# Attention and FP4 FFN kernel: the FFN input of two tiles is quantized as one, block-transposed on VectorE and moved by transfers

## The chip, the core and the metric

The kernel runs on one core of one Trainium2 chip, as one launch. The metric is the device time of that launch in microseconds (us). Three runs before the change took 3573.21, 3571.87 and 3572.76 us; the median is 3572.76 us.

## What is computed

The reference is one transformer block on 8 sequences of 1024 rows and 512 columns, in float32. A layer norm, causal attention in a latent form (16 heads of 32 columns, 16 further columns that are rotated by position) and a residual sum come first. Then come a second layer norm and a gated FFN of 1408 hidden columns, of which every input and every weight is rounded to a 4-bit grid with one scale for each 16 consecutive columns:

```
def fp4_quant_dequant(x):
    xb = x.reshape(shape[:-1] + (shape[-1] // BLOCK, BLOCK))     # BLOCK = 16
    scale = jnp.max(jnp.abs(xb), axis=-1, keepdims=True) / 6.0
    scale = jnp.maximum(scale, jnp.float32(1e-12))
    idx = jnp.searchsorted(_MID, jnp.abs(xb / scale))
    q = _GRID[idx] * jnp.sign(xb / scale) * scale
...
gate = fp4_linear(x, w_gate)
y = fp4_linear(x, w_up)
h = jax.nn.silu(gate) * y
return fp4_linear(h, w_down)
...
x = x + attention(layernorm(x))
x = x + ffn(layernorm(x))
```

## The kernel before

**Two streams of work.** Attention runs in 16 units of 512 rows (two per sequence, four tiles of 128 rows each). An even unit has three score steps per group of four heads, an odd unit seven, and there are four groups. `score_step` (L577) lays the matmuls of one step, ScalarE's exponentials (L618), the clamp of the first half on VectorE (L633) and of the second on GpSimd (L636), and for steps on the diagonal the causal mask on GpSimd (L640). The sums over steps are made on VectorE (L662). At the end of a unit `out_proj` (L779) multiplies by w_o, which `fetch_wo` (L775) loads anew each time into a buffer that score steps use too, adds x and writes the tile to a buffer in DRAM (`mid`).

The FFN runs in 32 pairs of two tiles. Of pair m: `fetch` (L813) loads y, one tile at a time, from `mid`; `begin` (L817) takes the norm's statistics; `scaled` (L822) norms a tile on ScalarE and queues its quantization; `turned` (L828) turns a tile with four matmuls against an identity matrix (L835) and ScalarE copies the result into two yT tiles (L840). Then six `gate` and six `up` pieces (L861, L881) run over the hidden columns, 256 at a time and 128 in the last, with yT as the moving operand (L853); `down` (L901) multiplies the quantized h by w_down and `finish` (L923) adds the residual and stores.

**Quantization.** `quantize` (L201) takes parts of up to 512 columns: a block maximum (L214), six small operations on the scales (L230 to L235), and per part six passes (L254, L262, L265, L268 twice, L250). With `turned` set, as for h, whose blocks of 16 lie along the partitions, it also transposes blocks of 32 x 32 on VectorE before and after (L224).

**Attention's own input** already goes another way in most units: `settle` (L390) transposes 32 x 32 blocks of xp on VectorE (L393) and 16 transfers of 32 partitions move the blocks to their places in xnT (L398). The planner counts 13 us for them.

**Order.** TensorE, VectorE and ScalarE run in the order in which the source lays instructions (`manual_schedule`, L78); GpSimd and SP, which issues nearly all transfers, are ordered by the framework's scheduler. The class `Clock` keeps the author's estimates of each engine's time. `slack` (L132) queues VectorE's quantization steps, `fill` puts them where the planner expects VectorE to be idle, and `need` (L102) forces the steps of one key out.

`ffn_pieces` (L930) is a list of pieces, each with a cost. A unit takes pieces up to a budget and spreads them between its score steps; units 13 and 14 have 22 us taken off their budget:

```
budget = within * (13, 5)[u % 2 == 0] / left
if u in (n_units - 3, n_units - 2):
    budget -= 22.0
```

What is left goes to unit 15. Pair 30 and pair 31 need unit 15's output, so they, and most of pair 29, run after all attention; that stretch is called the tail here. yT and h tiles share a ring of nine buffers, and y tiles have two.

Of the kernel before, what the change touches and what calls it, by code (L numbers as in the profile page):

```python
# [18 lines left out]
P = 128  # L19
# [23 lines left out]
def tile_mla_then_fp4_ffn(  # L43
# [31 lines left out]


    ET = mybir.EngineType
    ctx.enter_context(tc.manual_schedule(engines={ET.PE, ET.DVE, ET.Activation}))  # L78

    class Clock:  # L80

# [92 lines left out]
    xls.update({t: load_x(0, t, p2, "y") for t in range(2, NT)})  # L174
    by_chunk = lambda w: w.rearrange("(c p) n -> p c n", p=P)
    by_head = lambda w: w.rearrange("p (h n) -> p h n", n=64)
    of_four = lambda w: w.unsqueeze(0).to_broadcast([4, *w.shape])
# [20 lines left out]
        on_act(0.56, lambda: nc.scalar.copy(dst, pt[:, 0:n, :]))  # L198


    def quantize(parts, key, turned=False, ready=0.0):  # L201

        ends, at = [], 0
        for part in parts:
# [30 lines left out]
            nc.vector.reciprocal(rs, sc)  # L235

        for k, part in enumerate(parts):
            if turned:
                turn_blocks(part)
            slack(0.06 + 0.0012 * part.shape[1], lambda k=k: amax(k), key, ready=ready)  # L240
        slack(1.1 + 0.008 * nb, scales, key)
        for part, end in zip(parts, ends):
            step, bl = part.shape[1], slice(*end)
            nbl = step // BLK
            part3 = part.rearrange("p (b k) -> p b k", k=BLK)

            def times(which, part3=part3, bl=bl, nbl=nbl):
                by = got[which][:, bl].unsqueeze(2).to_broadcast([P, nbl, BLK])
                if which == "sc":
                    nc.vector.tensor_tensor(part3, part3, by, ALU.mult)  # L250
                else:


                    nc.vector.scalar_tensor_tensor(  # L254
                        part3, part3, BELOW_ONE, by, ALU.mult, ALU.mult
                    )

            def steps(part=part, step=step):  # L260
# [12 lines left out]
            slack(pass_cost, lambda f=to_grid: f(ALU.add), key)  # L273
            slack(pass_cost, lambda f=to_grid: f(ALU.subtract), key)
            slack(pass_cost, lambda f=times: f("sc"), key)
            if turned:
                turn_blocks(part)


# [297 lines left out]
    def score_step(u, hq, j, qc, qr, acc, aT):  # L577
# [46 lines left out]
        while silus:  # L624
            silus.popleft()()

        for k, (half, ready) in enumerate(zip(halves, done)):
            part = pT[:, half, :cols]
            if k == 0:
                on_dve(  # L630
                    0.1 + 0.00062 * wide,
                    ready,
                    lambda: nc.vector.tensor_scalar(part, part, E_HI, E_LO, ALU.min, ALU.max),  # L633
                )
            else:
                nc.gpsimd.tensor_scalar(part, part, E_HI, E_LO, ALU.min, ALU.max)  # L636
            if masked:

                diag = pT[:, half, : len(segs) * P].rearrange("p h (n k) -> p h n k", k=P)
                nc.gpsimd.affine_select(  # L640
                    out=diag,
                    in_=diag,
                    pattern=[[0, 2], [0, len(segs)], [1, P]],
                    compare_op=ALU.is_ge,
                    fill=0.0,
                    base=0,
                    channel_multiplier=-1,
                )
        ready = clk.act + 0.4 + 0.0009 * wide + (0.7 if masked else 0.0)


# [158 lines left out]
    NS = (NFC + 1) // 2  # L810
    ys, yTs, hs, ends = {}, {}, {}, {}

    def fetch(n):  # L813
        ys[n] = p2.tile([P, D], F32, tag="y", name=f"y_{n}")
        nc.sync.dma_start(out=ys[n], in_=mids[tiles[n]])

    def begin(*ns):  # L817
        for n in ns:
            stats, ends[n, "y"] = normed(ys[n], ("y", n))
            slack(0.9, stats, ("ny", n), True, clk.pe + 2.0)  # L820

    def scaled(n):  # L822
        clk.need(("ny", n), pe=False)
        clk.act = max(clk.act, clk.done["ny", n] + 2.5)
        on_act(0.65, ends.pop((n, "y")))
        quantize([ys[n]], ("y", n), ready=clk.act)

    def turned(n):  # L828
        m, t = divmod(n, 2)
        clk.need(("y", n))  # L830
        if t == 0:
            yTs[m] = [ring.tile([P, 2, 256], F32, tag="h", name="yT") for _ in range(2)]
        pt = bank("pt").rearrange("p (n k) -> p n k", k=P)
        for i in range(NDC):
            nc.tensor.transpose(pt[:, i, :], ys[n][:, i * P : (i + 1) * P], ident)  # L835
            clk.pe += 0.11
        ys.pop(n)
        for i in range(2):
            to = yTs[m][i][:, :, t * P : (t + 1) * P]
            on_act(0.38, lambda: nc.scalar.copy(to, pt[:, 2 * i : 2 * i + 2, :]))  # L840

    def hidden(m, w, k):

        n = min(2, NFC - 2 * k)
        pg = bank("pg").rearrange("p (n k) -> p n k", k=256)[:, :n]
        for c in range(n):
            f0 = (2 * k + c) * P
            for i in range(NDC):
                mm(
                    pg[:, c, :],  # L850
                    lhsT=w[:, i, f0 : f0 + P],
                    rhs=yTs[m][i // 2][:, i % 2, :],
                    start=(c == 0 and i == 0),  # L853
                    stop=(c == n - 1 and i == NDC - 1),
                    skip_group_check=True,
                )
        return pg
# [1 line left out]
    flat = lambda x: x.rearrange("p n k -> p (n k)")  # L859

    def gate(m, k):  # L861
        pg = hidden(m, wg_T, k)
        if k == 0:
            hs[m] = []
        if k < NS - 1:
            h = ring.tile([P, 2, 256], F32, tag="h", name="h")
        else:
            h = p1.tile([P, 1, 256], F32, tag="h_last", name="h")
        hs[m].append(h)
        copy_out(h, pg)  # L870
        if k % 2 == 1:

            def silu(hk=hs[m][k - 1 :]):
                for h in hk:
                    on_act(0.2 + 0.0009 * h.free_size(), lambda: nc.scalar.activation(h, h, AF.Silu))
                clk.silu = clk.act
                clk.act += 2.6

            silus.append(silu)

    def up(m, k):  # L881
# [8 lines left out]
        )  # L890
        for group in ((0, 1), (2, 3), (4,), (5,)) if m == pairs - 1 else ((0, 1), (2, 3), (4, 5)):
            if k == group[-1]:
                quantize([flat(hs[m][j]) for j in group], ("h", m, k // 2), True)
        if k == NS - 1:
            yTs.pop(m)

# [33 lines left out]
    def ffn_pieces():  # L930

        last = pairs - 1
        for t in range(2):
            yield 0.0, t, lambda t=t: fetch(t)
        for t in range(2):
            yield 1.0, t, lambda t=t: begin(t)
        for t in range(2):
            yield 1.0, t, lambda t=t: scaled(t)
        for t in range(2):
            yield 0.5, t, lambda t=t: turned(t)  # L940
        cost = lambda k: 3.5 if k < NS - 1 else 1.8
        for m in range(pairs):
            n = 2 * m + 1
# [6 lines left out]
            if m > 0:  # L950
                yield 0.0, n, lambda m=m: fetch_x1(2 * m - 2)
            if m < last:
                yield 0.0, n + 2, lambda n=n: fetch(n + 1)
                yield 0.0, n + 2, lambda n=n: fetch(n + 2)
            yield from run(gate, 1)
            if m < last:
                yield 0.0, n + 2, lambda n=n: begin(n + 1, n + 2)
            yield from run(up, 0, 1)
            if m < last:
                yield 0.0, n + 2, lambda n=n: scaled(n + 1)  # L960
            if m > 0:
                yield 9.6, n, lambda m=m: down(m - 1, (0,))
                yield 9.6, n, lambda m=m: down(m - 1, (1,))
            if m < last:
                yield 0.0, n + 2, lambda n=n: scaled(n + 2)
            yield from run(gate, 2, 3)
            yield from run(up, 2, 3)
            yield from run(gate, 4, 5)
            if m < last:
# [28 lines left out]
    for u in range(n_units):  # L998
# [8 lines left out]
        if u < FIRST:  # L1007
# [4 lines left out]
            for _ in range(8 if u == FIRST - 1 else 0):  # L1012
                c, n, run = ffn.popleft()
                take.append((c, run, n))
        else:
# [103 lines left out]
```

## Time and profile before

| What | Value |
|---|---|
| median of three runs | 3572.76 us |
| the profiled execution: its own time, its span | 3574.26 us, 3572.5 us |
| mean granted TensorE clock | 0.997 |
| transfers on SP's queue (q1): packets, share of 16 engines | 187780, 13.5% |
| yT<-pt copies on ScalarE (L840), x128 | 41.4 us, 377 ns each |
| FFN gate, up and down matmuls, busy | 640.3, 639.7 and 617.9 us |
| VectorE busy from 800 to 1000 us | 91.09 and 91.82 us of each 100 |
| SP waiting for the turning matmuls (L835) before it loads y | 566.8 us, 47 times |

How to read it: the profile is one execution with every instruction timed. Busy time is the union of an engine's instructions. A line such as `L835 PE MATMUL pt<-ident,y ... x256 | 39.3, 276 | 0.1` gives the source line, engine, operation, what it writes and reads, the count, the busy us, the mean ns of one, and the idle us of the engine just before. One matmul in the program shows as two records for float32, a transpose as one. SP's busy time is not shown, since it only issues; its issues stand in the timeline.

### The profile page before, as it was taken

Reading aid. Unit: us, or ns where it says so; the run is one execution under the profiler, and the core shown is the slowest. Engines: PE = TensorE matmul, PEld = TensorE weight load, DVE = VectorE, ACT = ScalarE, POOL = GpSimd, SP = SyncE. Lnnn points to the kernel's source line nnn. Section 1 sums busy time; section 2 is a strip of 40 time slices with the busy share of each in tenths; the row PEclk is TensorE's granted clock in tenths of the full one; section 3 lists DMA queues with packets and bytes.
Section 4 is the critical chain, followed back from the end, with each engine's and each line's share of the span. In section 5 each row is a group of like instructions: output and inputs, shape, how many; then the busy total and the mean of one; then the engine's idle time right before and its main releaser. Section 6 shows DMA issues by size and latency. Waiting matters only on the chain.

```text
span 3572.5 us, 50383 instructions
## 1 busy us (share of the span) xinstructions
PE 3508.8 (98%) x19700; PEld 2016.3 (56%) x19700; DVE 2911.5 (81%) x5308; ACT 1327.7 (37%) x1850; POOL 769.6 (22%) x1086
## 2 busy tenths in 40 slices
PE   8999999999999999999999999999999999999999
PEld 4334355556655555555566555565556655555576
DVE  6778659789977889887989778898878886779987
ACT  4444443333333333333333333333343433343311
POOL 3333322112121121221221211212222122122100
PEclk9999999999999999999999999999999999999999
DMA  3212111111021101111110211011111102100100
GB/s 93 72 45 73 46 40 48 45 34 30 19 62 30 60 18 30 43 53 45 32 28 19 62 30 54 24 30 41 52 45 30 30 24 60 42 18 19 54 30 15
DMA packets 189865, 145.17 MB, mean 41 GB/s; under 512 B 126524, under 2 KB 128060, under 8 KB 189628
## 3 DMA queue, kind: packets, MB, share of 16 engines
q1 hardware_dynamic: 187780, 141.09, 13.5%
q8 instruction: 155, 2.54, 0.3%
q10 hardware_dynamic: 1848, 0.87, 0.1%
q14 instruction: 82, 0.67, 0.1%
HBM read 94.72 MB, written 33.55 MB: 36 GB/s over the span
## 4 chain that ended last, share of the span: by engine, by line
PE 70%; DVE 13%; ACT 1%; issue 1%; POOL 1%; DMA 1%; SPq 0%; ACTq 0%; DVEq 0%; POOLq 0%
PE pg L117 29%; PE pd L117 14%; PE sc_ps L117 9%; PE po L117 5%; PE num L117 5%; DVE pT L662 2%; PE pp L117 2%; DVE h L268 1%; PE den L117 1%; PE pv L117 1%; DVE h L224 1%; PE pqr L117 1%; PE pk L117 1%; PE pq L117 1%; DVE rs L214 1%
## 5 line engine op out<-in xcount | busy, mean ns | idle before, releaser
L618 ACT ACTIVATE pT<-sc_ps 128x1024 f32<-128x1024 f32 (+1 forms) x640 | 565.9, 936 | 1108.5 <-PE sc_ps L117 1009.8
L117 PE MATMUL pg<-yT,wg_T 128*128 128x256 f32 x2816 | 640.3, 382 | 1.0 <-ACT yT L840 1.0
L117 PE MATMUL pg<-yT,wu_T 128*128 128x256 f32 x2816 | 639.7, 381 | 0.0
L117 PE MATMUL pd<-wd_T,h 128*128 128x512 f32 x1408 | 617.9, 594 | 2.0 <-DVE h L224 2.0
L117 PEld LDWEIGHTS pg<-yT,wg_T 128*128 128x128 f32 x2816 | 528.6, 190 | 133.1 <-issue 44.5
L117 PEld LDWEIGHTS pg<-yT,wu_T 128*128 128x128 f32 x2816 | 527.3, 190 | 110.9 <-issue 32.0
L636 POOL TENSOR_SCALAR pT<-pT 128x1024 f32<-128x1024 f32 (+1 forms) x320 | 338.3, 1057 | 1083.5 <-ACT pT L618 928.5
L640 POOL TENSOR_SCALAR_AFFINE_SELECT pT<-pT 128x256 f32<-128x256 f32 (+1 forms) x384 | 239.3, 623 | 1302.9 <-DVE pT L633 975.5
L662 DVE TENSOR_TENSOR pT<-pT 128x1024 f32<-128x1024 f32 (+3 forms) x528 | 468.3, 916 | 6.9 <-POOL pT L640 3.5
L117 PEld LDWEIGHTS pd<-wd_T,h 128*128 128x128 f32 x1408 | 265.0, 190 | 339.3 <-issue 319.3
L633 DVE TENSOR_SCALAR pT<-pT 128x1024 f32<-128x1024 f32 (+1 forms) x320 | 208.1, 650 | 210.8 <-ACT pT L618 209.4
L130 ACT COPY h<-pg 128x512 f32<-128x512 f32 x192 | 105.5, 550 | 656.4 <-PE pg L117 656.4
L117 PE MATMUL sc_ps<-qc,kT 32*128 32x512 f32 (+3 forms) x3072 | 338.3, 525 | 9.3 <-ACT pT L618 9.2
L117 PE MATMUL num<-pT,v 128*32 128x512 f32 (+3 forms) x3072 | 328.9, 497 | 13.1 <-POOL pT L640 12.9
L117 PE MATMUL sc_ps<-qr,kr 32*128 32x512 f32 (+3 forms) x3072 | 305.6, 482 | 5.3 <-DVE qr L552 5.3
L268 DVE TENSOR_TENSOR h<-h,m 128x512 f32<-128x512 f32 (+1 forms) x384 | 263.5, 686 | 10.1
L889 DVE TENSOR_TENSOR h<-pg,h 128x512 f32<-128x512 f32 x192 | 123.3, 642 | 165.0 <-PE pg L117 159.8
L224 DVE STREAM_TRANSPOSE h<-h 128x512 f32<-128x512 f32 (+1 forms) x384 | 250.6, 658 | 4.9
L117 PE MATMUL po<-wo,aT 128*128 128x512 f32 x512 | 229.1, 606 | 11.4 <-DMA wo<-in_w_o_dram 9.8
L117 PEld LDWEIGHTS sc_ps<-qc,kT 32*128 32x128 f32 x3072 | 114.3, 183 | 189.9 <-issue 129.1
L117 PEld LDWEIGHTS sc_ps<-qr,kr 32*128 32x128 f32 x3072 | 144.1, 185 | 110.9 <-issue 78.5
L117 PEld LDWEIGHTS num<-pT,v 128*32 128x32 f32 x3072 | 67.9, 108 | 225.9 <-issue 127.1
(97 smaller groups left out, 3606.8 us busy)
## 6 DMA issues: line engine op xcount, KB each, us to landing
xo<-in_x_dram SPq DMA_DIRECT2D x64, 256.0 KB, 2.7
wo<-in_w_o_dram SPq DMA_DIRECT2D x16, 1024.0 KB, 5.3
mid<-xo SPq DMA_DIRECT2D x64, 256.0 KB, 2.1
y<-mid SPq DMA_DIRECT2D x64, 256.0 KB, 2.7
xr<-mid SPq DMA_DIRECT2D x64, 256.0 KB, 2.6
out_dram<-xr SPq DMA_DIRECT2D x64, 256.0 KB, 2.0
xp<-in_x_dram SPq DMA_DIRECT2D x30, 512.0 KB, 3.7
xnT<-xp SPq DMA_DIRECT2D x416, 32.0 KB, 2.0
```

Source lines behind the costliest of these rows:

```text
L117: nc.tensor.matmul(dst, **kw)
L130: on_act(0.1 + 0.0009 * src.free_size(), lambda: nc.scalar.copy(dst, src))
L214: nc.vector.tensor_reduce(got["rs"][:, slice(*ends[k])], parts[k].rearrange("p (b k) -> p b k", k=BLK), AX.X, ALU.max, apply_absolute_valu ...
L224: 0.06 + 0.0013 * part.shape[1], lambda: nc.vector.transpose(part, part), key
L268: nc.vector.tensor_tensor(part, part, got["m"], op)
L618: lambda: nc.scalar.activation(part, sc[:, 2 * k : 2 * k + 2, :cols], AF.Exp, scale=SM_SCALE),
L633: lambda: nc.vector.tensor_scalar(part, part, E_HI, E_LO, ALU.min, ALU.max),
L636: nc.gpsimd.tensor_scalar(part, part, E_HI, E_LO, ALU.min, ALU.max)
L640: nc.gpsimd.affine_select(out=diag, in_=diag, pattern=[[0, 2], [0, len(segs)], [1, P]], compare_op=ALU.is_ge, fill=0.0, base=0, channel_mu ...
L662: lambda a=whole, b=part: nc.vector.tensor_tensor(a, a, b, ALU.add),
L889: lambda: nc.vector.tensor_tensor(h, pg, h, ALU.mult),
```

## The change

A pair's y is one tile of [128, 2 halves of columns, 2 tiles, 256], in a single buffer. Both tiles are scaled by one piece and quantized by one call over the two halves, so the small scale operations run once a pair. With "last" in `turned`, each half ends with VectorE's block transposes. In place of `turned`, `moved` issues 16 transfers for each half, which put the blocks at their places in the two yT tiles; four matmuls and two copies per tile are gone. `moved` stands after the third up piece, where `turned` stood after the last gate piece and after the fifth up piece. The ring's h tiles of steps 2 to 4 are claimed together, so that yT comes behind them in the ring.

GpSimd joins the engines that run in the source's order; within a diagonal score step its clamp comes first and the two masks after, the second half's ahead of the first's. The two budgets lose 40 us where they lost 22, and the first unit with FFN work takes the four pieces that now stand for the eight. x tiles 2 and 3 of the first unit are loaded into one tile of the new shape.

```
-    ctx.enter_context(tc.manual_schedule(engines={ET.PE, ET.DVE, ET.Activation}))
+    ctx.enter_context(tc.manual_schedule(engines={ET.PE, ET.DVE, ET.Activation, ET.Pool}))
...
-            if turned:
+            if "first" in turned:
                 turn_blocks(part)
...
-            if turned:
+            if "last" in turned:
                 turn_blocks(part)
...
+                def mask(diag=diag):
+                    nc.gpsimd.affine_select(
...
+                masks.append(mask)
+        while masks:
+            masks.pop()()
...
-    def scaled(n):
-        clk.need(("ny", n), pe=False)
-        clk.act = max(clk.act, clk.done["ny", n] + 2.5)
-        on_act(0.65, ends.pop((n, "y")))
-        quantize([ys[n]], ("y", n), ready=clk.act)
-    def turned(n):
-        m, t = divmod(n, 2)
-        clk.need(("y", n))
...
-        for i in range(NDC):
-            nc.tensor.transpose(pt[:, i, :], ys[n][:, i * P : (i + 1) * P], ident)
...
-            on_act(0.38, lambda: nc.scalar.copy(to, pt[:, 2 * i : 2 * i + 2, :]))
+    def scaled(m):
+        clk.need(("ny", m), pe=False)
+        clk.act = max(clk.act, clk.done["ny", m] + 2.5)
+        for t in range(2):
+            on_act(0.65, ends.pop((m, t, "y")))
+        halves = [ys[m][:, c].rearrange("p t n -> p (t n)") for c in range(2)]
+        quantize(halves, ("y", m), ("last",), clk.act)
+    def moved(m):
+        clk.need(("y", m), pe=False)
+        rows = ys.pop(m).rearrange("p h t (c q k) -> p h (t c) q k", q=4, k=32)
+        yTs[m] = []
+        for c in range(2):
+            yT = ring.tile([P, 4, P], F32, tag="h", name="yT")
+            for a in range(4):
+                for q in range(4):
+                    nc.sync.dma_start(
+                        out=yT[32 * q : 32 * q + 32, :, 32 * a : 32 * a + 32],
+                        in_=rows[32 * a : 32 * a + 32, c, :, q, :],
+                    )
+            yTs[m].append(yT.rearrange("p (t c) k -> p c t k", t=2))
+        arrive[m] = max(clk.pe, clk.done["y", m]) + 13.0
...
             if m < last:
-                yield 0.0, n + 2, lambda n=n: scaled(n + 1)
+                yield 0.0, n + 2, lambda m=m: scaled(m + 1)
             if m > 0:
                 yield 9.6, n, lambda m=m: down(m - 1, (0,))
                 yield 9.6, n, lambda m=m: down(m - 1, (1,))
+            yield from run(gate, 2, 3)
+            yield from run(up, 2)
             if m < last:
-                yield 0.0, n + 2, lambda n=n: scaled(n + 2)
-            yield from run(gate, 2, 3)
-            yield from run(up, 2, 3)
+                yield 0.0, n + 2, lambda m=m: moved(m + 1)
+            yield from run(up, 3)
             yield from run(gate, 4, 5)
-            if m < last:
-                yield 0.5, n + 2, lambda n=n: turned(n + 1)
-            yield from run(up, 4)
-            if m < last:
-                yield 0.5, n + 2, lambda n=n: turned(n + 2)
-            yield from run(up, 5)
+            yield from run(up, 4, 5)
...
-                budget -= 22.0
+                budget -= 40.0
```

More of the change, by code (lines that the diff above doesn't have):

```diff
@@ L173, in tile_mla_then_fp4_ffn @@
         nc.sync.dma_start(out=xls[t], in_=x[0, t * P : (t + 1) * P, :])
-    xls.update({t: load_x(0, t, p2, "y") for t in range(2, NT)})
+    other = p1.tile([P, 2, D], F32, tag="y", name="x_0_1")
+    xls.update({t: other[:, t - 2, :] for t in range(2, NT)})
+    for t in range(2, NT):
+        nc.sync.dma_start(out=xls[t], in_=x[0, t * P : (t + 1) * P, :])
     by_chunk = lambda w: w.rearrange("(c p) n -> p c n", p=P)
@@ L198, in turn, with quantize @@
         on_act(0.56, lambda: nc.scalar.copy(dst, pt[:, 0:n, :]))
-    def quantize(parts, key, turned=False, ready=0.0):
+    def quantize(parts, key, turned=(), ready=0.0):
         ends, at = [], 0
@@ L625, in score_step @@
             silus.popleft()()
+        masks = []
         for k, (half, ready) in enumerate(zip(halves, done)):
@@ L639, in score_step @@
                 diag = pT[:, half, : len(segs) * P].rearrange("p h (n k) -> p h n k", k=P)
[L640 to L648, printed above, removed]
+                def mask(diag=diag):
+                    nc.gpsimd.affine_select(
+                        out=diag,
+                        in_=diag,
+                        pattern=[[0, 2], [0, len(segs)], [1, P]],
+                        compare_op=ALU.is_ge,
+                        fill=0.0,
+                        base=0,
+                        channel_multiplier=-1,
+                    )
+                masks.append(mask)
+        while masks:
+            masks.pop()()
         ready = clk.act + 0.4 + 0.0009 * wide + (0.7 if masked else 0.0)
@@ L811, in tile_mla_then_fp4_ffn @@
     ys, yTs, hs, ends = {}, {}, {}, {}
[L813 to L820, printed above, removed]
-    def scaled(n):
-        clk.need(("ny", n), pe=False)
-        clk.act = max(clk.act, clk.done["ny", n] + 2.5)
-        on_act(0.65, ends.pop((n, "y")))
-        quantize([ys[n]], ("y", n), ready=clk.act)
@@ L828, in turned, with fetch @@
-    def turned(n):
-        m, t = divmod(n, 2)
-        clk.need(("y", n))
-        if t == 0:
-            yTs[m] = [ring.tile([P, 2, 256], F32, tag="h", name="yT") for _ in range(2)]
-        pt = bank("pt").rearrange("p (n k) -> p n k", k=P)
-        for i in range(NDC):
[L835 to L839, printed above, removed]
-            on_act(0.38, lambda: nc.scalar.copy(to, pt[:, 2 * i : 2 * i + 2, :]))
+    def fetch(m):
+        ys[m] = p1.tile([P, 2, 2, 256], F32, tag="y", name=f"y_{m}")
+        for t in range(2):
+            nc.sync.dma_start(
+                out=ys[m][:, :, t, :],
+                in_=mids[tiles[2 * m + t]].rearrange("p (c n) -> p c n", c=2),
+            )
@@ new lines, in begin @@
+    def begin(m):
+        for t in range(2):
+            stats, ends[m, t, "y"] = normed(ys[m][:, :, t, :], ("y", m, t))
+            slack(0.9, stats, ("ny", m), True, clk.pe + 2.0)
+    def scaled(m):
+        clk.need(("ny", m), pe=False)
+        clk.act = max(clk.act, clk.done["ny", m] + 2.5)
+        for t in range(2):
+            on_act(0.65, ends.pop((m, t, "y")))
+        halves = [ys[m][:, c].rearrange("p t n -> p (t n)") for c in range(2)]
+        quantize(halves, ("y", m), ("last",), clk.act)
@@ new lines, in moved @@
+    def moved(m):
[6 more added lines that the diff above has]
+                for q in range(4):
+                    nc.sync.dma_start(
+                        out=yT[32 * q : 32 * q + 32, :, 32 * a : 32 * a + 32],
+                        in_=rows[32 * a : 32 * a + 32, c, :, q, :],
+                    )
+            yTs[m].append(yT.rearrange("p (t c) k -> p c t k", t=2))
+        arrive[m] = max(clk.pe, clk.done["y", m]) + 13.0
@@ L842, in hidden @@
+    arrive = {}
     def hidden(m, w, k):
@@ L849, in hidden @@
                 mm(
-                    pg[:, c, :],
+                    pg[:, c, :].rearrange("p (t k) -> p t k", t=2),
                     lhsT=w[:, i, f0 : f0 + P],
-                    rhs=yTs[m][i // 2][:, i % 2, :],
+                    rhs=yTs[m][i // 2][:, i % 2],
                     start=(c == 0 and i == 0),
@@ L861, in gate, with silu @@
     def gate(m, k):
-        pg = hidden(m, wg_T, k)
         if k == 0:
             hs[m] = []
[L865 to L869, printed above, removed]
+            there = arrive.pop(m)
+            clk.pe = max(clk.pe, there)
+        pg = hidden(m, wg_T, k)
+        for _ in range({0: 1, 1: 1, 2: 3}.get(k, 0)):
+            hs[m].append(ring.tile([P, 2, 256], F32, tag="h", name="h"))
+        if k == NS - 1:
+            hs[m].append(p1.tile([P, 1, 256], F32, tag="h_last", name="h"))
+        h = hs[m][k]
         copy_out(h, pg)
         if k % 2 == 1:
-            def silu(hk=hs[m][k - 1 :]):
+            def silu(hk=hs[m][k - 1 : k + 1]):
                 for h in hk:
@@ L892, in up @@
             if k == group[-1]:
-                quantize([flat(hs[m][j]) for j in group], ("h", m, k // 2), True)
+                quantize([flat(hs[m][j]) for j in group], ("h", m, k // 2), ("first", "last"))
         if k == NS - 1:
@@ L932, in ffn_pieces @@
         last = pairs - 1
[L933 to L940, printed above, removed]
+        yield 0.0, 1, lambda: fetch(0)
+        yield 1.0, 1, lambda: begin(0)
+        yield 1.0, 1, lambda: scaled(0)
+        yield 4.0, 1, lambda: moved(0)
         cost = lambda k: 3.5 if k < NS - 1 else 1.8
@@ L952, in ffn_pieces @@
             if m < last:
-                yield 0.0, n + 2, lambda n=n: fetch(n + 1)
-                yield 0.0, n + 2, lambda n=n: fetch(n + 2)
+                yield 0.0, n + 2, lambda m=m: fetch(m + 1)
             yield from run(gate, 1)
             if m < last:
-                yield 0.0, n + 2, lambda n=n: begin(n + 1, n + 2)
+                yield 0.0, n + 2, lambda m=m: begin(m + 1)
             yield from run(up, 0, 1)
             if m < last:
-                yield 0.0, n + 2, lambda n=n: scaled(n + 1)
+                yield 0.0, n + 2, lambda m=m: scaled(m + 1)
             if m > 0:
@@ L1010, in tile_mla_then_fp4_ffn @@
                 take.append(weight_work.popleft())
-            for _ in range(8 if u == FIRST - 1 else 0):
+            for _ in range(4 if u == FIRST - 1 else 0):
                 c, n, run = ffn.popleft()
```

## The prediction

> **What bounds the kernel now.** I read the page's first rows, then who TensorE waited for, then stretches of the timeline.
>
> ```profile
> PE 3508.8 (98%) x19700; PEld 2016.3 (56%) x19700; DVE 2911.5 (81%) x5308; ACT 1327.7 (37%) x1850; POOL 769.6 (22%) x1086
> ```
>
> TensorE is idle for 3572.5 - 3508.8 = 63.7 us of the span. A busy record need not mean full speed, so I look at spacing. In the timeline, start us and duration come first:
>
> ```profile
> 1242.73 5.45 PE L117 MATMUL pg<-yT,wg_T 128*128 128x256 f32 x24
> 1248.02 0.60 PE L835 MATMUL pt<-ident,y 128*128 128x128 f32 x4
> 1248.45 3.62 PE L117 MATMUL pg<-yT,wu_T 128*128 128x256 f32 x16
> ```
>
> Groups start where the one before has issued its last matmul: 16 FFN matmuls take 3.55 us (1248.45 to the next group's start at 1252.00). Steady work has no holes, so TensorE's own work sets the time. A rule speaks against this: the Trainium skill, "Perfetto Trace Analysis", Identifying the Most-Contended Engine, says that matmul busy time misjudges how close TensorE is to its peak, and to go by weight loads. By that (56%) TensorE has 44% of room and removing its work would bring about nothing; by the rows the order of work leaves it 2% idle, and what it issues is time. I go by the rows for the bound, but take the rule's reason, pipelining, for the size: a group's busy time overstates what its removal saves.
>
> The waits (us in total, times, longest):
>
> ```profile
> PE num L117 <- POOL pT L640: 12.9, 14, 1.8
> PE po L117 <- DMA wo<-in_w_o_dram: 9.8, 3, 5.5
> PE sc_ps L117 <- ACT pT L618: 9.2, 18, 1.6
> ...
> PE pr L117 <- DMA xnT<-xp: 2.7, 1, 2.7
> ```
>
> Those on L640 and L618 are nearly all in the first 500 us. The wo and xnT waits lie near the end, in units 13 to 15.
>
> **Part 1: the transposes leave TensorE (gain).** There are 64 groups of four (L835).
>
> ```profile
> L835 PE MATMUL pt<-ident,y 128*128 128x128 f32 x256 | 39.3, 276 | 0.1
> ...
> L393 DVE STREAM_TRANSPOSE xp<-xp 128x512 f32<-128x512 f32 x52 | 33.8, 687 | 2.8 <-ACT xp L348 2.8
> ```
>
> The row says 39.3 us, but that counts the tail that overlaps the next group. From start to next start the groups shown take 1248.45 - 1248.02 = 0.43, and others 0.50 (1255.92 to 1256.42) and 0.44 (3486.21 to 3486.65): 0.45 x 64 = 28.8 us. Bounds: 0.43 x 64 = 27.5 and 39.3. I take 28.8, all on the path. ScalarE also loses 128 copies x 0.377 = 48 us; at 37% busy that is worth nothing by itself.
>
> **Part 2: VectorE (nothing).** Added: 64 block transposes of 512 columns, priced by L393: 64 x 0.687 = 44.0 us. Removed: the six small scale operations run once per pair. By shape they take 1.455 us a set on 32 blocks (0.353 + 0.253 + 0.252 + 0.213 + 0.192 + 0.192) and 1.84 on 64, so 64 x 1.455 - 32 x 1.84 = 34.2 us. Net 9.8 us on an engine with 660 us idle. Cover is thin only from 3150 to 3400, where VectorE is 92 to 96% busy; there it gains about 1%. If that cover fails, all 9.8 us count.
>
> **Part 3: the 32 transfers per pair (small loss).** SP now issues 31 x 32 = 992 more transfers for pairs 1 to 31, and 32 for pair 0, each 32 partitions x 4 runs of 128 B. The nearest row is xnT, with 8 runs each:
>
> ```profile
> 1235.37 10.40 SPq L398 DMA_DIRECT2D xnT<-xp  x16
> 1247.20 0.39 SPq L363 DMA_DIRECT2D xp<-in_x_dram  x1
> ```
>
> Sixteen take 10.40 us, 0.65 apiece, landing 2.0 us later. Low bound: 0.32 (mid stores, 128 runs of 2 KB). I take 0.65, since source, partitions and run length are xnT's. A rule weighs in against the change: the Trainium skill, "DMA: Bandwidth & Descriptors", Rules for kernel authors, calls transfers below 64 KB mostly overhead and advises against a plain transfer with a rearranged pattern as a transpose (19x). The page's fixed price, about 2.0 us each (Anatomy of one DMA, for another issuing path), would make an estimate of 64 us per pair if nothing overlapped; no pair has such a gap before its first gate, so TensorE would stand for 25 to 50 us per pair, over 750 us in all. By the row they overlap: 32 x 0.65 + 2.0 = 22.8 us. I use the row.
>
> Is that hidden? Before, from the last y multiplication (L250) to the pair's first gate matmul there are 14.5 us (pairs 7, 12, 17), 15.7 to 16.1 (1, 5, 10, 15, 20), 19.0 (31), and 20 to 39 else. In the changed order y's last block transpose stands on VectorE before the multiplication of the third or fourth up step; before, in pairs 1, 7, 12, 17, it came before the fifth. I add TensorE's work from the preceding up step to the first gate (0.435 us per FFN matmul of the program, 0.868 per down matmul, about 1 us per four attention ones) and take off VectorE's work in between. Pairs 7, 12, 17 become 38.6 us; 5, 10, 15, 20 become 20.1; pair 1 has 16.9; 31, whose sum falls 6 us short of the trace when made for before, about 17. The first half's 16 transfers need only the first half, which ends 4.3 to 7.2 us of VectorE work earlier. So the last transfer lands 20.8 - 4.3 + 2.0 = 18.5 us after y's end at most. Short by about 1.5 us: pairs 1 and 31. Pairs 8, 13 and 18 have 16 xnT transfers inside their batch (+10.4 = 28.9) against sums of 27.7 that run some 3 us high: 3 x about 2 us. Expected loss 4 us with ends 0 and 25 (the latter if gaps also pull the clock down).
>
> Behind a batch that waits for VectorE, SP holds y loads, outputs, xo loads and wo. The y load follows the landed batch and precedes the use by two gates. For wo of the last units the sums leave 21.6, 24.9 and 18.7 us from y's end to po; it stands after 14, 22 and 32 transfers, so it lands about 10.5, 15 and 21.5 us after. Only the last, before the tail, is short by up to 3 us; I count 1 us in the tail's uncertainty. The wait of 566.8 us of SP for L835 goes away; nobody waited on it.
>
> **Part 4: the planner's 40 (gain).** Counted in the two orders, unit 13 loses 32 FFN matmuls, unit 14 loses 24 and unit 15 gains 56: 24 us of work moves later. What matters is where it lands: before po in unit 14 there was none and now 16 (7 us), in unit 15 8 and now 16. The chain shows the place:
>
> ```profile
> 2940.44 0.83 PE num L117 x8
> 2941.27 0.02 issue
> 2941.28 5.31 DMA wo<-in_w_o_dram
> 2946.59 0.14 issue
> 2946.72 16.71 PE po L117 x32
> ```
>
> The 5.5 and 3.9 us waits for wo fit under 7 us. The 32 po matmuls then take 16.71 us instead of 32 x 0.434 = 13.9, and 17.00 after the second wait, since the clock falls: 2.8 and 3.1 us more. Up to 15.3 us go, and the xnT wait of 2.7 us (its gap grows from 13 to 20 us by the sums). Against that: unit 14 has less to hide attention's waits, and VectorE is densest in unit 15. Ends -3 and 20; I take 12.
>
> **Part 5: GpSimd in source order (nothing).** In place of mask, clamp, mask it runs clamp (1.057 us), mask, mask (0.623 each). Before, it sat behind VectorE's clamp for 975.5 us; now its own clamp starts as soon as ScalarE is done, but the first half's mask comes last, 0.6 us later. A quarter to one microsecond either way on at most 14 waits: I take 0, ends -6 and 6. Its norm operations now stand where the source has them, behind VectorE's bn_aggr, with the next clamp behind them; two gates pass before they are due.
>
> **Sum.** The profiled execution took 3574.26 us, span 3572.5. Minus 28.8, minus 12, plus 4: 3537.5. The median of the runs is 1.5 lower: 3536.
>
> **The rivals.**
> A, the sum: 3536, between 3524 and 3548. Chance 0.60.
> B, only the transposes count: the late gain is eaten by new waits in units 14, 15 and the tail, and 12 us more of transfers are late. 3572.8 - 28.8 + 12 = 3556, between 3548 and 3565. For it: VectorE near 95% from 3150 on. Against it: TensorE showed no wait there with the same ratio of work. Chance 0.26.
> C, slower: the transfers take 22.8 us after y's end with no overlap of the halves, at the distances of before, less 1.4 us for the two added block transposes. Shortfalls against 24.3 us over the 31 pairs add up to 91 us, 10 of them of 4 us and more, which at about 3 us of lost clock each add 30. 3572.8 - 28.8 + 121 = 3665; with half of the 121, 3604. It decides from a mean stall of 28.8 / 31 = 0.93 us per pair. For it: SP issues strictly in order, and pairs sit behind waits for VectorE. Against it: y's end moves ahead of the fourth up step in the changed order. Chance 0.08.
> D, no difference: the gains are cancelled within 7 us. 3572. Chance 0.06.
>
> **Numbers.** 0.2% (7 us) is about what a measurement of this kernel can tell from no change. Faster: A and B, 0.86; same: D, 0.06; slower: C, 0.08. The low end takes the late part at 20, no late transfers, GpSimd's gain 6: -55, 3518; I cut it to 3520. The high end covers B: 3564.
>
> **What would show it.** The L835 rows are gone and TensorE has 256 matmuls fewer. yT transfers appear x1024, near 0.65 us; at 0.4 all pairs are in time. A wait of PE pg for DMA yT tells part 3: under 8 us means A, over 30 C. Waits for wo fall from 9.8 to under 3 and the clock shows 1.0 around 2940 and 3100 if part 4 is right. VectorE's busy time rises about 10 us. I am wrong if pg waits often, or if TensorE begins to wait for VectorE in unit 15.

## The result and the profile after

The changed kernel takes 3579.93 us (median of 12 runs, 3576.41 to 3583.4), the kernel before 3572.26 us beside it (12 runs, 3569.98 to 3574.23). The ratio is 1.0024, 95% interval 1.0016 to 1.0031: slower by some 8 us, where the prediction said 36 us faster. The profiled execution took 3579.62 us, with a span of 3577.8 us; the mean granted clock was 0.996.

The page's first row:

```profile
PE 3479.2 (97%) x19444; PEld 1988.6 (56%) x19444; DVE 2924.0 (82%) x5180; ACT 1288.0 (36%) x1722; POOL 764.6 (21%) x1086
```

TensorE's busy time fell by 3508.8 - 3479.2 = 29.6 us. That this is nearly the 28.8 us forecast for the transposes is in part luck, as Part 1 below works out. Its idle time rose from 63.7 to 3577.8 - 3479.2 = 98.6 us. The transposes are gone, and more time than they took came back as holes. Who TensorE waited for (us in total, times, longest) says where they are:

```profile
PE pg L117 <- DMA yT<-y: 22.5, 6, 5.9
PE num L117 <- POOL pT L645: 17.7, 21, 3.9
...
PE pd L117 <- DVE h L227: 10.4, 9, 1.7
...
PE pg L117 <- issue: 2.5, 2, 2.0
...
PE po L117 <- DMA wo<-in_w_o_dram: 0.8, 2, 0.7
```

Three things are new. Gate matmuls wait 22.5 us for yT, which is the new transfers' wait. The wait of down (pd) for the quantized h rose from 2.0 to 10.4 us, and that of num for GpSimd from 12.9 to 17.7. The wait for wo is down from 9.8 to 0.8 as forecast.

The page's row of transfers, KB each and median us from issue to landing, shows 1024 of them:

```profile
yT<-y SPq DMA_DIRECT2D x1024, 16.0 KB, 1.8
```

One takes SP 0.599 us in the median, so neither the price (0.65) nor the landing (2.0) was misjudged. What was misjudged in the first place is when a batch starts. Pair 1, in the timeline of all engines (start us, us; brackets hold the idle time before a row):

```profile
543.30 10.51 SPq L401 DMA_DIRECT2D xnT<-xp  x16
...
547.11 0.70 DVE L227 STREAM_TRANSPOSE y<-y 128x512 f32<-128x512 f32 x1
...
551.52 0.71 DVE L227 STREAM_TRANSPOSE y<-y 128x512 f32<-128x512 f32 x1
...
553.93 21.38 SPq L854 DMA_DIRECT2D yT<-y  x32
...
569.92 1.03 PE L117 MATMUL pg<-yT,wg_T 128*128 128x256 f32 x4
...
576.89 3.33 PE L117 MATMUL pg<-yT,wg_T 128*128 128x256 f32 x7 [5.94 <-DMA yT<-y]
```

The first half of y was ready at 547.81 and the second at 552.23, but SP was handing out the 16 xnT transfers until 553.81. All 32 then came in one row of 21.4 us, none of them beside VectorE's work on the second half. TensorE used the first yT tile at 569.92 (four matmuls) and stood until the second had landed.

In pairs 8, 13 and 18 the xnT batch falls in the middle: in pair 8, SP issued 20 of the 32 from 1235.22 to 1249.05, then 16 for xnT, then the other 12 from 1259.59 to 1267.29. These pairs waited 2.43, 2.21 and 2.00 us.

Some of the gaps also lower the clock. The answer by windows gives, for a stretch, us, busy time of PE, PEld, DVE, ACT and POOL with counts, granted clock, DMA share and GB/s. The changed kernel around pair 1:

```profile
540.00:600.00 60.00, 53.99 (x322) 36.16 (x319) 45.93 (x84) 26.93 (x37) 11.79 (x19) 0.94 0.20 44
```

The same 60 us in the version of experiment e6 below, which differs in these transfers (and in GpSimd's part):

```profile
540.00:600.00 60.00, 59.54 (x378) 39.41 (x371) 57.15 (x106) 29.52 (x41) 17.56 (x29) 1.00 0.25 53
```

In 60 us the changed kernel has 322 matmul records against 378: a wait of 5.94 us and a clock of 0.94 cost some 9 us of progress (56 records of 0.16 us).

Two traces side by side allow a stricter reading. The changed kernel and the version of e8 below, which differs from it in these transfers alone, have the same 19444 TensorE records in the same order, so the lateness of each record can be taken from the two traces. It grows by 9.4 us at pair 1 (from 568 to 640 us), by 2.7, 2.4 and 3.9 us at pairs 8, 13 and 18, by 4.5 us just before unit 15's end, by 2.3 us at 3433 us (where the profile names "issue") and by 8.0 us at pair 31: 33 of the 37 us by which the last record is late. No other pair adds more than 1 us at its gates; of the rest, 2.0 us come between 2773 and 2800 us, in waits for VectorE.

### The profile page after: what moved, and what is told of

It reads as the page before. It is cut to its first block, busy times and chain, and to the rows that moved or that the text cites. A ratio compares the mean times of both kernels' runs of the same rounds, so it can differ in the third digit from the quotient of the medians.

```text
span 3577.8 us, 51047 instructions
## 1 busy us (share of the span) xinstructions
PE 3479.2 (97%) x19444; PEld 1988.6 (56%) x19444; DVE 2924.0 (82%) x5180; ACT 1288.0 (36%) x1722; POOL 764.6 (21%) x1086
## 3 DMA queue, kind: packets, MB, share of 16 engines
q8 instruction: 154, 2.52, 0.3%
## 5 line engine op out<-in xcount | busy, mean ns | idle before, releaser
L640 POOL TENSOR_SCALAR pT<-pT 128x1024 f32<-128x1024 f32 (+1 forms) x320 | 337.6, 1055 | 2301.1 <-ACT pT L621 2169.0
L117 PE MATMUL pg<-yT,wg_T 128*128 128x256 f32 x2816 | 648.2, 385 | 25.0 <-DMA yT<-y 22.5
L117 PE MATMUL pd<-wd_T,h 128*128 128x512 f32 x1408 | 621.1, 596 | 10.4 <-DVE h L227 10.4
L672 DVE TENSOR_TENSOR pT<-pT 128x1024 f32<-128x1024 f32 (+3 forms) x528 | 458.7, 897 | 22.3 <-POOL pT L645 19.0
L637 DVE TENSOR_SCALAR pT<-pT 128x1024 f32<-128x1024 f32 (+1 forms) x320 | 219.2, 685 | 202.9 <-ACT pT L621 199.6
L117 PE MATMUL sc_ps<-qc,kT 32*128 32x512 f32 (+3 forms) x3072 | 339.0, 526 | 12.6 <-ACT pT L621 12.6
L117 PE MATMUL num<-pT,v 128*32 128x512 f32 (+3 forms) x3072 | 315.4, 497 | 20.1 <-POOL pT L645 17.7
L271 DVE TENSOR_TENSOR h<-h,m 128x512 f32<-128x512 f32 (+1 forms) x384 | 259.2, 675 | 10.4
```

The lines of the kernel that those rows point to most:

```text
L117: nc.tensor.matmul(dst, **kw)
L672: lambda a=whole, b=part: nc.vector.tensor_tensor(a, a, b, ALU.add),
```

## The experiments

Theory T: the 32 transfers of a pair are late, and late transfers ate the gains. Rivals: GpSimd's order did it, or the planner's 40 filled the tail. Each part was first done alone, then the transfers were varied with everything else kept.

**e1, GpSimd's part alone**, on the kernel before.

```
+ manual_schedule(engines={ET.PE, ET.DVE, ET.Activation, ET.Pool})
+ masks collected, issued after both clamps, the second half's first
```

> The kernel of before with GpSimd in the source's order and its clamp ahead of the two masks, and nothing else of the change. Theory T (the gain of 28.8 us is eaten by late yT transfers, 24.5 us of waits and some 5 us of lowered clock, and GpSimd's order is a side matter): 3577, 2 to 8 us slower than before, since in the changed kernel the waits of the score products for GpSimd's mask rose from 12.9 to 17.7 us. Rival G (GpSimd's order is what eats the gain, by blocking clamps behind norm operations that wait for VectorE and by making VectorE's sums late): 3590 or more. No effect, as I predicted: within 3 us of before.

3579.9 us (3572.85 before; ratio 1.0019, 1.0012 to 1.0026): 7.0 us slower. This part, counted at nothing, costs as much by itself as the whole change does, but it does not explain why the gains are missing.

**e2, the budget alone**, on the kernel before: `budget -= 40.0` where it was 22.

> The kernel of before with 40 in place of 22 in the two budgets and nothing else. Theory T: the late part's gain is real without the transfers, the waits for wo in units 14 and 15 go and with them the lowered clock: 8 to 15 us faster than before, about 3561. Rival B (moving FFN work into unit 15 and next to the tail costs as much as it gains, because VectorE is full there): within 3 us of before or slower.

3559.61 us, ratio 0.9964 (0.995 to 0.9977): a gain of 13.2 us, with the waits for wo at 0.8 us. Part 4 was forecast at 12.

**e3, the move alone**: the changed kernel without GpSimd's part and with 22. **e4**, the same with 40.

> The changed kernel with GpSimd left to the scheduler, the masks in their old order and the budgets at 22: quantizing, turning and moving of y alone. Theory T: the transfers are late in the same places (pair 1, pairs 8, 13, 18, the tail), TensorE waits 15 to 30 us for yT, and the time is 5 to 15 us above before, because the gain of 28.8 us is eaten and the late part's gain is missing: about 3582. Rival G: without GpSimd's order the transposes' gain stands, 3545 to 3555.

> The changed kernel with GpSimd left to the scheduler and the masks in their old order; transfers and budgets of 40 stay. Theory T: 3 to 8 us faster than the changed kernel, about 3574, waits for yT still over 15 us. Rival G: 3550 or less.

e3 took 3576.63 us, ratio 1.0013 (1.0006 to 1.0019); e4 3574.83 us, ratio 1.0006 (0.9998 to 1.0014). So the move, which takes 28.8 us of work off TensorE, is a loss by itself, and beside it the budget brings 1.8 us in place of 13.2. In e3, TensorE waited 18.0 us for yT, 10.4 for h and 13.1 for GpSimd's pT (12.9 before). The wait for yT and the longer wait for h belong to the move; the longer one for GpSimd does not.

**e5, two plain transfers per pair.** The changed kernel whole, with one transfer of 128 partitions for each half. It leaves out moving blocks between partitions and keeps all other work, so it prices the 32 transfers and their lateness.

```
-            for a in range(4):
-                for q in range(4):
-                    nc.sync.dma_start(out=yT[32 * q ...], in_=rows[32 * a ...])
+            nc.sync.dma_start(out=yT, in_=plain[:, c])
```

> The changed kernel with two transfers of 128 partitions per pair in place of 32; they leave out the moving of blocks between partitions, so the result is not the reference's, and all other work is the same. Theory T (the 32 transfers are late, and the waits for yT and the lowered clock behind them are most of what eats the gain): no wait of TensorE for yT over 1 us, 3545 to 3553, that is about 30 us below the changed kernel. Rival V (VectorE's new order, with down waiting for h and score products for GpSimd, is most of it): waits for yT vanish but the time stays above 3565.

3542.12 us, ratio 0.9917 (0.9903 to 0.993): 37.8 us less than the changed kernel. The waits for yT are gone, the others stand. Its page:

```profile
PE 3466.8 (98%) x19444; PEld 1982.0 (56%) x19444; DVE 2925.7 (83%) x5180; ACT 1288.4 (36%) x1722; POOL 763.3 (22%) x1086
```

Against the changed kernel its idle time fell from 98.6 to 3540.0 - 3466.8 = 73.2, by 25.4 us: the waits for yT, 22.5, and most of those named "issue", 2.5. Its busy time fell by 12.4 us with the same 19444 matmul records in the same order, and the mean clock rose from 0.996 to 0.999, which alone would make about 0.003 x 3479 = 10 us. About a third of the price of being late is therefore paid after the wait, in matmuls at a lower clock.

**e6, the whole computation with 10 transfers per pair.** e4, with each half written to DRAM by 4 transfers that put the blocks in place, and read back by 1.

```
+            turned = dram.tile([P, 4, P], F32, tag="yt", name=f"yt_{m}_{c}")
+            there = turned.rearrange("(q r) j (a k) -> a r j q k", q=4, a=4)
             for a in range(4):
-                for q in range(4):
-                    nc.sync.dma_start(out=yT[32 * q ...], in_=rows[32 * a ..., c, :, q, :])
+                nc.sync.dma_start(out=there[a], in_=rows[32 * a : 32 * a + 32, c])
+            nc.sync.dma_start(out=yT, in_=turned)
```

> GpSimd left to the scheduler as in e4, budgets of 40, and each half moved by four transfers into a buffer in DRAM and one back: ten per pair in place of 32, all of the computation kept. By the rows: ten issues of about 0.65 us, one landing of about 2.1 and one of 2.7 us, about 8 us after y's end in place of 18.5. Theory T: no waits for yT but in the tail, 3540 to 3552. Rival V: within 10 us of e4, 3565 to 3575.

3538.99 us, ratio 0.9907 (0.9893 to 0.9921): the fastest version, ahead of both kernels. It moves the data twice, yet is 35.8 us faster than e4. Its batch in pair 1, by SP's timeline, behind the same xnT batch:

```profile
542.59 10.51 SPq L401 DMA_DIRECT2D xnT<-xp  x16
553.20 3.94 SPq L848 DMA_DIRECT2D yt<-y  x6
...
560.99 0.33 SPq L849 DMA_DIRECT2D yT<-yt  x1
```

The batch starts as late as in the changed kernel, but its last issue ends at 561.32, not 575.31. At nearly the same price for each issue, their number sets the length.

**e7, the same 32 transfers placed earlier**: in e4, `moved` stands one gate and one up piece ahead of its place.

```
-            yield from run(gate, 2, 3)
-            yield from run(up, 2)
+            yield from run(gate, 2)
             if m < last: yield ... moved(m + 1)
-            yield from run(up, 3)
+            yield from run(gate, 3)
+            yield from run(up, 2, 3)
```

> As e4, but the moving piece stands two pieces earlier, after the third gate piece; 7 us of FFN matmuls more lie between it and the next pair's first gate. Theory T: waits for yT fall from 22.4 to under 10 us, with pair 1 and the tail left, and the time to about 3560; VectorE's queue is pressed earlier, so down's wait for h may grow. Rival V: that wait grows by as much as is gained, 3570 or more.

3595.88 us, ratio 1.0066 (1.0053 to 1.0078): slower still, and neither theory had said so. The waits of e7:

```profile
PE po L117 <- DVE xo L799: 12.8, 1, 12.8
PE po L117 <- DMA wo<-in_w_o_dram: 12.3, 3, 7.3
...
PE pg L117 <- DVE xo L799: 8.4, 1, 8.4
PE pg L117 <- DMA yT<-y: 7.3, 2, 5.9
```

The wait for yT fell from 22.4 to 7.3 us, as it should, but two single waits of together 21.2 us came in pair 1, and the wait for wo, 1.7 us in e4, grew to 12.3. For the first, VectorE's work on y came ahead of the addition (L799) that w_o's next matmuls needed. The second shows in SP's timeline:

```profile
537.26 21.52 SPq L847 DMA_DIRECT2D yT<-y  x32
...
561.19 0.60 SPq L163 DMA_DIRECT2D xo<-in_x_dram  x1
```

The load of xo stood behind the batch until 561.19; VectorE waited 14.96 us for it. The loads of wo near the end stood behind such batches too:

```profile
2921.11 20.99 SPq L847 DMA_DIRECT2D yT<-y  x32
2942.21 0.52 SPq L780 DMA_DIRECT2D wo<-in_w_o_dram  x1
```

Moved forward, the batch makes late whatever is queued behind it.

**e8, e6 with GpSimd's part**, which is the changed kernel with its transfers alone exchanged.

> The changed kernel whole, GpSimd in the source's order included, but each half of a pair goes by way of DRAM: 4 transfers out in turned places and 1 back, 10 per pair in place of 32. The earlier run of these 10 transfers without GpSimd's order took 3538.99 us. Theory (GpSimd's order has a price of its own, wherever the transfers stand): 5 to 7 us more, 3544 to 3546; TensorE waits for pT of GpSimd 17.7 us where it waited 14.0, none for yT. Rival (its price came about only with late transfers): 3539, the same as without.

3542.69 us, ratio 0.9916 (0.9903 to 0.993). It is 37.2 us under the changed kernel, the price of the 32 transfers with the computation whole. It is 3.7 us over e6, so GpSimd's part costs something here too, nearer to 4 than to the 5 to 7 expected.

**e9, e6 without VectorE's 64 block turns of y.** Their places in the order are kept, the turns left out.

```
-  lambda: nc.vector.transpose(part, part), key
+  lambda: None if key[0] == "y" else nc.vector.transpose(part, part), key
```

> The 10 transfers by way of DRAM without GpSimd's order (3538.99 us), and VectorE's 64 block turns of y are left out, the order of everything else kept; so the blocks of y stay unturned and the FFN's input is wrong by that. 64 x 0.71 us = 45 us of VectorE's work go. Theory V (the wait of down for h, 10.4 us where before had 2.0, comes from the work that the change put on VectorE): the wait falls to some 2 us, time 3530 to 3533. Rival W (TensorE arrives sooner by the transposes that it lost, and h is as late as ever): the wait stays near 10 us, time 3537 to 3540.

3536.3 us, ratio 0.9899 (0.9885 to 0.9912), 2.7 us under e6. VectorE's busy time fell from 2920.0 to 2881.4 us, and the wait of pd for h stayed at 10.4 us, nine times, 1.7 at the longest.

VectorE's added work is not what makes h late. That leaves the order in VectorE's queue and TensorE's earlier arrival. Both can be seen where the wait comes. Before (timeline of all engines, the rows of one place):

```profile
1365.42 0.45 DVE L235 RECIPROCAL rs<-sc 128x48 f32<-128x48 f32 x1
...
1368.84 0.69 DVE L331 BATCH_NORM_STATS2 ny<-y 128x6 f32<-128x512 f32 x1
...
1370.38 8.75 PE L117 MATMUL pd<-wd_T,h 128*128 128x512 f32 x20
...
1379.72 1.12 PE L117 MATMUL pd<-wd_T,h 128*128 128x512 f32 x2 [0.59 <-DVE h L224]
```

And in e6:

```profile
1364.60 0.69 DVE L334 BATCH_NORM_STATS2 ny<-y 128x6 f32<-128x512 f32 x1
...
1365.84 7.03 PE L117 MATMUL pd<-wd_T,h 128*128 128x512 f32 x16
...
1367.35 0.45 DVE L238 RECIPROCAL rs<-sc 128x48 f32<-128x48 f32 x1
...
1374.59 1.99 PE L117 MATMUL pd<-wd_T,h 128*128 128x512 f32 x4 [1.72 <-DVE h L227]
```

The reciprocal ends the scales of h's last parts. Before, it ran ahead of the norm's statistics of y and 5 us ahead of the first down matmul; in the new order it runs behind them and 1.5 us after down has begun. The statistics themselves stand 1.5 us ahead of down before and 1.2 us in e6, so by these rows it is the order that moved the reciprocal, and hardly TensorE's earlier arrival. No run puts the order back, so this is read from rows and not shown by an experiment. The wait of 1.72 us shown and one of 0.84 at 1377.41 come in four pairs.

**e10, GpSimd in the source's order, the masks left where they were**, on the kernel before.

> The kernel before with GpSimd in the source's order, but the masks left where they were, each ahead of the next half's clamp, not collected and issued backwards after both. Before with both edits took 3579.9 us against 3572.9. Theory (the fixed order is what costs, since what waits at the head of GpSimd's queue holds up work that could go): 3578 to 3582. Rival (the masks' place costs): 3572 to 3574.

3571.0 us against 3571.84, ratio 0.9997 (0.9989 to 1.0005). The rival holds: the fixed order alone is free, and under it, it is the masks' new place that costs. TensorE's own wait for GpSimd says little of how: 12.9 us in e10 and 15.7 in e1. VectorE's sums over the steps (L662 in e10, L669 in e1) wait for the masks too. From VectorE's lists in e10 and, after it, in e1:

```profile
DVE pT L662 <- POOL pT L640: 3.5, 5, 2.0
```

```profile
DVE pT L669 <- POOL pT L642: 19.0, 27, 3.6
```

Where the time goes can be read by comparing TensorE's records in the two traces, 19700 in nearly the same order. At 500 us, with most of the waits for GpSimd past, e1 is only 0.7 us late; at 2900 us it is 3.4 us late, at 3000 us 8.2, at the end 7.5. In the steepest stretch TensorE waits for VectorE's h (the rows of e10 and, after it, of e1):

```profile
2924.91 2.84 PE L117 MATMUL pv<-wuv,ckv 128*128 128x512 f32 x6 [2.32 <-DVE h L889]
```

```profile
2930.37 5.36 PE L117 MATMUL pv<-wuv,ckv 128*128 128x512 f32 x6 [4.17 <-DVE h L896]
```

The wait is 1.85 us longer, and the same six matmul records take 2.52 us more. That VectorE is late here because its sums waited for the masks is likely, but it is argued from these rows and not shown by a run.

**e11, the 32 transfers on two queues**: e4, every second one issued from GpSimd's queue.

```
-                    nc.sync.dma_start(
+                    (nc.sync if q % 2 else nc.gpsimd).dma_start(
```

> The change without GpSimd's order (3574.8 us, 22.4 us of waits for yT); of the 32 transfers of a pair every second one is issued from GpSimd's queue in place of SP's, the work being the same. Theory (SP's issue, 0.60 us for each, sets the length of a batch): a batch takes some 10 us, the waits for yT fall under 5 us, time 3540 to 3550, as far as GpSimd's clamps are not held up. Rival D (the DMA engines set it, with their many short runs): a batch still takes 19 us, waits for yT stay at 18 to 25 us, time 3570 to 3578. Rival G (GpSimd's own work is late behind 16 issues): waits for pT of GpSimd grow from 14 us to over 25, time over 3560.

3560.55 us, ratio 0.9968 (0.9956 to 0.9979): 14.3 us under e4, and 21.6 over e6. TensorE's list has no wait for yT left. The batch of pair 1 in SP's timeline:

```profile
556.29 10.75 SPq L847 DMA_DIRECT2D yT<-y  x16
```

The batch is half as long, so the issuing queue sets its length and rival D falls. The hoped-for 3540 to 3550 was missed all the same: GpSimd spends 285.4 us more on issuing. Of the waits the one for qr grew from 5.7 to 9.1 us against e6, that for wo to 2.5, that for GpSimd from 14.0 to 15.7, which is not the 25 of rival G, and 3.5 us for h are new. These are some 11 us; the rest of the 21.6 is not traced.

**e12, e6 with 22.**

> The 10 transfers by way of DRAM without GpSimd's order (3538.99 us), with the budget back at 22. Alone the budget of 40 gained some 13 us; beside the 32 late transfers it gained 2 (3576.63 to 3574.83). Theory (the 32 transfers ate its gain at the end of the kernel, where they were late too): the budget is worth its full 12 to 13 us here, time 3550 to 3553, waits for wo 9 to 10 us. Rival (the move of y itself takes the gain away, whatever its transfers): 2 us, time 3540 to 3543.

3553.37 us, ratio 0.9945 (0.9931 to 0.9959). The medians side by side, without GpSimd's part:

| | budget 22 | budget 40 | the 40 brings |
|---|---|---|---|
| as before | 3572.85 | 3559.61 | -13.2 |
| move, 32 transfers | 3576.63 | 3574.83 | -1.8 |
| move, 10 transfers | 3553.37 | 3538.99 | -14.4 |
| 32 less 10 | 23.3 | 35.8 | |

The budget keeps its worth beside the move as such; beside the 32 transfers it loses it. The traces show where. In e3 and e12, and in e4 and e6, TensorE's 19444 records come in the same order, so the lateness that the 32 transfers bring can be followed under each budget:

| lateness with 32 against 10 transfers, us | at 2900 us | grown by 3340 us | by 3366 us | in the tail | at the end |
|---|---|---|---|---|---|
| budget 22 (e3 against e12) | 15.4 | -2.6 | -0.2 | +10.6 | 23.2 |
| budget 40 (e4 against e6) | 16.1 | +1.7 | +5.9 | +10.4 | 34.1 |

Up to 2900 us and in the tail the two budgets pay alike. Around 3000 us, with 22, both kernels wait for wo and xnT, the one with 10 transfers somewhat longer (5.53 us for 5.19, 2.52 for 1.49) and with slower matmuls behind, so the late one makes up 2.6 us. With 40, e4 waits 1.71 us for wo there and e6 0.25. Ahead of unit 15's end, e4 waits 4.51 us for yT at 3349.79, and its next 12 gate records then take 4.51 us; e3 stands for 0.69 us at that place, and the same 12 take 2.83 us. These two places make 10.4 of the 10.9 us between the profiled executions (12.6 between the medians).

## Why the prediction was wrong

**Part 1 was right.** The clean figure is that of e12, which has neither GpSimd's part nor late transfers: TensorE's busy time fell by 3508.8 - 3481.7 = 27.1 us. The 29.6 us of the changed kernel hold two more terms that nearly cancel by luck: the masks' new place took 12.0 us off the busy time at an unchanged clock (3508.8 to 3496.8 in e1, mostly in the num matmuls), and the lowered clock put 12.4 on (e5). As the prediction read it, the rule on weight loads of the Trainium skill, "Perfetto Trace Analysis", Identifying the Most-Contended Engine, meant that nothing would come of it; the page speaks of how near TensorE is to its peak and not of what removing work saves. Once the transfers are in time, the move alone is worth 19.5 us (3572.85 to 3553.37).

**Part 3 is the step that failed**: "Expected loss 4 us with ends 0 and 25". It measured 37.2 us (e8), beyond its bound too. The mechanism was named, and the length of a batch was right (21.4 us for 20.8); the term was mis-sized in four ways.
- The step's own shortfalls, twice about 1.5 us and three times about 2, add up to some 9 us; the 4 us were put down without a reason.
- The step took it that the first half's 16 transfers go out while VectorE works on the second, so that the last lands 18.5 us after y's end "at most". In pair 1 the xnT batch stood in SP's queue ahead of the batch; TensorE restarted 24.7 us after y's end (576.89 - 552.23), where the cover was 17.7 us (to 569.92; forecast 16.9). I had put xnT inside the batch for pairs 8, 13 and 18, where waits of 2.0 to 2.4 us each came as forecast, and had not looked for it ahead of pair 1's. The timeline of before has it there, ending at 552.36, just before y's last multiplication ends at 553.41:

```profile
541.95 10.41 SPq L398 DMA_DIRECT2D xnT<-xp  x16
```

- The cover at the end was too large. For pair 31 I took 17 us, after adding the 6 us by which the sum fell short when made for before. Its y ended at 3479.28, and TensorE ran out of work at 3490.58, 11.3 us later, about what the sum gives without the 6; the wait was 5.90 us. Before unit 15's end, 4.07 us came in a pair that I had counted as safe. The first comes under a budget of 22 too (5.88 us in e3); the second comes with 40 only, so parts 3 and 4 do not add up as two separate sums.
- The lowered clock was put in the upper end only. It came to 12.4 of the 37.8 us (e5).

**Part 4 was right by itself** (13.2 us for 12), and the signs that it named are there: no wait for wo to speak of, and around 2940 us a clock of 1.00 where it had been 0.91. Its gain was taken back by part 3, at the two places of e12's table.

**Part 5, counted at 0, cost 3.7 to 7.0 us** (e8 less e6, the changed kernel less e4 with 5.1, e1). The half to blame is the masks' place. The source's order, for which I had looked at norm operations behind VectorE, is free (e10). "A quarter to one microsecond either way on at most 14 waits" looked at TensorE's waits alone and left out VectorE's sums, whose wait for GpSimd rose from 3.5 to 19.0 us (e10, e1). The prediction's reading that the waits on L640 and L618 lie "nearly all in the first 500 us" was off too: 8.3 of 12.9 and 5.8 of 9.2 us do. What the masks' place costs without the source's order was not tried.

**Part 2 counted nothing for VectorE**, and its load is indeed worth little: 2.7 us for all 64 turns (e9). But the wait of down for h grew by 8.4 us, by the rows from order, not load. In e6 it comes near 886, 1375, 1864 and 2353 us, far from the stretch of 3150 to 3400 where I looked for trouble. I asked where VectorE is full, not which of its steps now stands ahead of another that TensorE needs. What in the planner put it there is not shown.

The books then nearly close: -28.8 for the transposes, -13.2 for the budget, +37.2 for the late transfers, some +5 for the masks and +8.4 for h give +8.6; measured +7.7. Two runs test the same terms with fewer of them: -28.8 and +8.4 give -20.4, where e12 measured -19.5; with -13.2 they give -33.6, where e6 measured -33.9. The 8.4 for h is a sum of waits, which no run isolates.

**The rivals.** C had the right place and, as it turned out, the right point: it decides from 0.93 us per pair, and the price was 37.2 / 31 = 1.2. Its sum of 121 us was too high, since six waits carried it, not 31 pairs. A and B left out most of the late transfers and the masks. D, no difference within 7 us, came nearest in size, but by cancelling that it did not name. The rules of the Trainium skill, "DMA: Bandwidth & Descriptors", Rules for kernel authors, against small and rearranged transfers pointed the right way. The estimate of over 750 us, made from the page's fixed price with no overlap, was twenty times too high: 32 transfers took 21.4 us of issuing. What made them bite was the number of issues on one queue.

## What to carry to other kernels

A batch of small transfers has a length, issues times the price of one, and this length stands in a queue: count what lies ahead of it at the moment when its data is ready, and what lies behind it. When work leaves the bounding engine, what it waits for is due earlier, and a gain moved to the end of the kernel shortens the cover of transfers there. When a batch is late, make fewer issues of it before moving it: going through DRAM with 10 transfers beat 32 direct ones by 36 us, while putting the 32 earlier cost 21.

## What the runs showed of the hardware

A transfer of 32 partitions cost SP about 0.6 to 0.66 us, whether it had 128 runs (yT in the changed kernel, 16 KB, 0.599), 256 (xnT, 32 KB, 10.51 / 16 = 0.66) or went out to DRAM with 64 KB (e6, 3.94 / 6 = 0.66); one of 256 KB from DRAM to 128 partitions cost 0.367 (e6). In these rows more bytes do not cost the issuing queue more. The shape can: a load of y, 256 KB from `mid`, cost SP 0.326 us before, when a row went to one place, and 0.582 us in the changed kernel, which puts a row's two halves in two places. Two queues issued side by side in e11, SP at 0.600 us and GpSimd at 0.548 us each.

A wait can cost more than itself. Three times 28 gate matmul records, by TensorE's timeline of the changed kernel:

```profile
1268.75 6.28 PE L117 MATMUL pg<-yT,wg_T 128*128 128x256 f32 x28 [2.43 <-DMA yT<-y]
...
2250.53 7.97 PE L117 MATMUL pg<-yT,wg_T 128*128 128x256 f32 x28 [2.00 <-DMA yT<-y]
...
3496.48 8.17 PE L117 MATMUL pg<-yT,wg_T 128*128 128x256 f32 x28 [5.90 <-DMA yT<-y]
```

After 5.90 us of idling they took 8.17 us, but after 2.00 us they took 7.97, and after the longer 2.43 us only 6.28. In the windows of 4 us the clock was 0.63 from 2250 to 2254, and it was not lowered around 1268. The length of the wait alone therefore does not decide; what does is not shown here.
